# One more batch of a first layer by Strassen's seven products: W1 loaded sooner, two groups of weight sums made later

## The chip, the cores and the metric

The kernel runs on one core of one Trainium2 chip. The metric is the device time of one execution in microseconds (us), as the median of several runs. The engines are named as in the profile: PE is TensorE's matrix multiply and PEld its weight load, DVE is VectorE, ACT is ScalarE, POOL is GpSimd and SP is SyncE, which issues most of the DMAs. A "q" behind a name (SPq, ACTq, POOLq) means the queue from which that engine issues DMAs.

## The reference

Eight batches of 256 tokens with 1024 features pass two layers, each added to its input. All is float32.

```python
# layer 0: mask holds 0 and 1, coeff is one number for each batch
x = x + (x @ W0.T + b0 + (x @ (2 * mask - 1)) * coeff)
# layer 1: a LoRA adapter of rank 16, picked for each batch by itok
x = x + (x @ W1.T + b1 + ((x @ A[itok]) @ B[itok]) * 2.0)
```

The mask differs from batch to batch, so layer 0 has a weight matrix of its own for each batch: W0.T + (2 mask - 1) coeff, with the identity added for the residual. Layer 1 has one weight matrix for all batches, W1.T plus the identity, and a small correction for each batch.

## The kernel before

**Two groups of four batches.** For each group the kernel runs the first layer of its batches one after the other, then the second layer of the whole group (`second_layer`, L613). The results y of a group stay in SBUF, features in rows.

**The first layer, plain.** The effective weights come in pieces of 256 input by 512 output features, eight to a batch. `load` (L171) sends a piece's mask on SP's queue (and W0 in batch 0, and a piece of x with some), four pieces ahead of use. `build` (L209) turns it into weights: one ACT activation computes (2 mask - 1) coeff (L227) and one DVE add puts W0 to it (L230), two pieces ahead of use. Masks have three buffers (pool "mask"), built pieces three as well (pool "weff"). `first_batch` (L271) and `first_layer` (L241) multiply: 64 matmuls of 128 by 128 by 256 for each batch, of which the profile counts two PE records each (L280, L255). Batches 0, 1, 2 and 3 go this way.

**The first layer by seven products.** Batches 4 to 7 (`SEVEN`, L20) use Strassen's method in Winograd's form, class `Seven` (L304): weights are cut in quarters a11, a12, a21, a22, tokens and inputs in halves. Four weight sums s1 to s4 and four token sums t1 to t4 stand in for one of eight quarter products. Each product is made in two halves of eight matmuls with 128 columns (L388), over three PSUM banks X, Y and Z. The order is X: a11; Y: a12; X: s2 t2; Z: s1 t1; X: s3 t3; Z: s4; X: a22 t4, and X and Z are read out between. ACT reads with the bias (L403), DVE adds the others (L408). `operands` (L344) lists the 20 steps that prepare a batch: four blocks a11, a11, a12, a12, then t1 and t2, then twice (a22, a21, s1, s2), then t3, s3 twice, s4 twice and t4. A weight sum is a DVE operation on 128 by 1024 elements (L326), a token sum two of 128 by 256 (L342). `run_one` (L469) keeps the operands ten steps ahead of the halves in the order of the program. The first three blocks of a batch lie in the three weff buffers, the others in pools T and q (L218 to L223).

**The second layer.** It is Strassen twice, one level inside the other: seven outer products A11, A12, S1, S2, S4, S3, A22 (`plan`, L780), each of seven inner products. Its left operands, the leaves, depend on W1 alone. `combine_weights` (L493) makes them in the first layer of group 0: a generator of DVE sums on 128 by 512 elements (L522 to L528, L539), of which `step` (L867) takes three or four after each piece. The leaves are written to HBM on POOL's queue (`keep`, L485) and read back on SP's, seven for each outer product (`load_leaves`, L622). W1's 16 blocks are loaded with the masks of pieces 10 to 21 (L206). The sums S3 are left over and made in the second layer of group 0 (`rest`, L559). `begin_adapters` and `load_adapters` bring the LoRA matrices.

**What sets the order.** The framework orders the instructions of each engine when the kernel is built: by the order of the program among those that it takes to be ready. The engines then keep to that order. `tc.issue_after(ins)` puts instructions behind a given one on its own engine; `behind(what)` does it for the instruction last noted under a name in `anchors`. SBUF pools give a buffer again when its last reader is done. The pools here: mask 3, weff 3, T 6, q 10, l 7 buffers.

```python
if b not in SEVEN or (h == 0 and g < 3):
    pool, tag = wpool, "w"
elif g >= NG // 2:
    pool, tag = tpool, "T"
else:
    pool, tag = qpool, "q"
```

Of the kernel before, what the change touches and what calls it, by code (L numbers as in the profile page):

```python
# [14 lines left out]
P = 128  # L15
# [3 lines left out]
BY_HALF = 3  # L19
SEVEN = (4, 5, 6, 7)  # L20
SCALING = 2.0
# [3 lines left out]
def kernel(  # L25
# [145 lines left out]
    def load(k: int):  # L171


        b, h, g = pieces[k]
        m_sb[k] = mpool.tile([P, 2, OH], I32, tag="m", name=f"m_{k}")
        pairs = [(m_sb[k], mask[b, g if b == 0 else h * NG + g])]
        if b == 0:
            pairs.append((w0_of(k), w0T[g]))
        x_pair = g // CG if b == 0 and g % CG == 0 else g if h == 0 else None
        if x_pair is not None:  # L180
            x = x_sb[b, x_pair] = xpool.tile([P, CG, T], F32, tag=f"x{x_pair}", name=f"x_{b}_{x_pair}")
        if k < BY_HALF:

            for i in range(2):
                for t, a in pairs:
                    nc.sync.dma_start(t[:, i], part(a, i))  # L186
                if k == 0 and i == 0:
                    nc.scalar.dma_start(x[:, 0], part(xT[0, 0], 0))
                elif k == 0:
                    nc.sync.dma_start(x[:, 1], part(xT[0, 0], 1))  # L190
                elif x_pair is not None and i == 0:
                    nc.sync.dma_start(x, xT[b, x_pair])
        else:
            for t, a in pairs:
                nc.sync.dma_start(t, a)
# [12 lines left out]

    def build(k: int):  # L209
# [94 lines left out]
    class Seven:  # L304
# [19 lines left out]
        def weight_sum(self, n, op, x, y, a):  # L324
            s = self.w[n, a] = qpool.tile([P, CG, OH], F32, tag="q", name=f"{n}_{self.b}_{a}")
            anchors["weights"] = op(s, self.w[x, a], self.w[y, a])  # L326
# [50 lines left out]
        def half(self, dest, left, right, a, first=False):  # L377
# [4 lines left out]
            for c in range(CG):  # L382
# [4 lines left out]
                for j in range(TPH):  # L387
                    nc.tensor.matmul(  # L388
                        ps[:, j, :],
# [17 lines left out]
        def add(self, i, v, ps):  # L407
            nc.vector.tensor_add(self.out(i, v), ps, self.out(i, v))  # L408

        def products(self):  # L410
# [38 lines left out]
    class Sevens:  # L449
# [43 lines left out]
    def combine_weights():  # L493
# [17 lines left out]
        def inner(name, blocks, own, place=None):  # L511
            a11, a12, a21, a22 = (blocks[u, v] for u in range(2) for v in range(2))
            s = {}
            for n in ("s1", "s2", "s3", "s4"):
                if place is None:
                    s[n] = lpool.tile([P, CG, OQ], F32, tag="l", name=f"{name}_{n}")
                else:
                    if n in ("s1", "s3"):
                        two = pair(f"{name}_{n}")
                    s[n] = two[:, n in ("s2", "s4")]  # L520
# [13 lines left out]

        def outer(name, op, x, y):
            tiles = [tpool.tile([P, 2, CG, OQ], F32, tag="T", name=f"{name}_{u}") for u in range(2)]
            out = {(u, v): tiles[u][:, v] for u in range(2) for v in range(2)}
            for uv in out:
# [74 lines left out]
    def second_layer(group: int, y, first, first_steps, second):  # L613
# [24 lines left out]
        def product(ps, l, r, first=False, by_tile=False):  # L638
            order = [(c, j) for c in range(CG) for j in range(2)]
            if by_tile:  # L640
                order.sort(key=lambda cj: cj[1])
            for c, j in order:
                nc.tensor.matmul(  # L643
                    ps[:, j, :],
                    lhsT=l[:, c, j * P : (j + 1) * P],
                    rhs=r[:, c, :],
                    start=first and c == 0 and j == 0,
                    stop=False,
                    skip_group_check=True,
                )  # L650

# [40 lines left out]
        def read(out, ps, other=None):  # L692
            if other is None:
                return nc.scalar.copy(out, ps)  # L694
            anchors["reads"] = nc.vector.tensor_add(out, ps, other)  # L695
            return anchors["reads"]
# [170 lines left out]
    def step(k: int):  # L867

        nonlocal sums
        if k == 2 * NG + 3:  # L870
            sums = combine_weights()
        with tc.issue_after(weff_at[min(k + BUILDS_AHEAD, max(weff_at))].ins):
            for _ in range(3 if k < 4 * NG + 2 else 4):
                next(sums, None)

    sevens = {g: Sevens([b for b in SEVEN if b // GB == g]) for g in range(NGROUP)}
    for group in range(NGROUP):
# [19 lines left out]
        for i in range(GB):  # L897
            if GB * group + i in SEVEN:
                continue
            between(GB * group + i)  # L900
            if group == 0 and i == 0:
                first_batch(y[0], step)
                continue
            for h in range(2):
                first_layer(GB * group + i, h, y[i][h], step)
                if group == 0 and i == 2 and h == 0:
                    late = y[i][h][:, 0, :1]
                    begin_adapters(late)
                    load_adapters(group, late)
        for _ in sums:  # L910
            pass
        anchors["layer"] = anchors["weights"]
# [75 lines left out]
```

## Time and profile before

| | |
|---|---|
| median of 3 runs | 410.01 us (409.81 to 411.64) |
| the profiled execution | 410.92 us, its span 409.1 us |
| first layer, group 0 | to 117.8 us in the span |
| second layer, group 0 | 117.8 to 211.4 us |
| first layer, group 1 | 211.4 to 312.0 us |
| second layer, group 1 | from 312.0 us |
| granted TensorE clock | 1.000 |
| DMA, mean | 238 GB/s; 395 GB/s from 60 to 118 us |
| mask, issue to landing, median | 9.2 us from 60 to 118 us, 4.4 us from 211 to 290 us |

The span is the time from the first to the last instruction of one profiled execution. A row of the chain or of the timeline begins with a start and a length in us, both counted from the span's start. "L255 PE MATMUL ps<-x,w ... x384" means 384 PE records of the matmul in line 255, which writes tile ps from x and w. A bracket behind a row gives the idle time of the engine ahead of it and what ended that. Busy time says that an engine had work, not that it set the time; for that the chain of work that ended last is read, which follows each step back to what released it.

### The profile page before, as it was taken

How to read it: one execution, taken by the hardware profiler on the slowest of the kernel's cores; microseconds unless marked ns; L12 is line 12 of the kernel's file. 1: busy time of each engine (PE TensorE's matmuls, PEld its weight loads, DVE VectorE, ACT ScalarE, POOL GpSimd, SP SyncE). 2: the span in 40 equal slices, each digit the busy share in tenths (PEclk: the TensorE clock that was granted, in tenths of full speed). 3: DMA queues.
4: the chain of work that ended last, by engine and by line, in shares of the span. 5: the costliest groups of instructions: out<-in, count | busy, mean ns of one | idle time of the engine just before them, and what ended most of it. 6: DMA issues, size and time to landing. Idle time of an engine off the chain costs nothing.

```text
span 409.1 us, 6555 instructions
## 1 busy us (share of the span) xinstructions
PE 403.8 (99%) x2458; PEld 358.2 (88%) x2458; DVE 300.7 (74%) x427; ACT 136.0 (33%) x213; POOL 38.6 (9%) x77
## 2 busy tenths in 40 slices
PE   8999999999999999999999999999999999999996
PEld 6888888888887888888899999999998788888885
DVE  2438598886647558994999999999936365886493
ACT  4434534543445201133115648174221420102200
POOL 0000042575201001000000000400000000000000
PEclk9999999999999999999999999999999999999999
DMA  8999799999987476767795758662122247554654
GB/s 274 405 402 387 274 371 414 412 393 331 414 331 256 134 234 199 220 218 201 241 367 162 263 184 302 202 215 96 26 74 66 75 145 230 173 154 162 213 154 154
DMA packets 41762, 97.44 MB, mean 238 GB/s; under 512 B 5508, under 2 KB 6276, under 8 KB 41732
## 3 DMA queue, kind: packets, MB, share of 16 engines
q1 hardware_dynamic: 32690, 76.17, 55.2%
q0 software_dynamic: 4288, 12.61, 8.1%
q10 hardware_dynamic: 4754, 8.26, 5.4%
q8 instruction: 19, 0.31, 0.3%
q14 instruction: 11, 0.09, 0.1%
HBM read 77.09 MB, written 19.92 MB: 237 GB/s over the span
## 4 chain that ended last, share of the span: by engine, by line
PE 91%; DMA 5%; ACT 2%; SPq 1%; DVE 0%; issue 0%; DVEq 0%; ACTq 0%
PE X L643 24%; PE ps L255 20%; PE X L388 12%; PE Z L643 12%; PE Z L388 6%; PE Y L643 6%; DMA m<-mask 5%; PE ps L280 4%; PE Y L388 3%; PE G L660 2%; PE psh L675 2%; ACT w L227 1%; ACT y L403 0%; SPq L186 0%; DVE w L230 0%
## 5 line engine op out<-in xcount | busy, mean ns | idle before, releaser
L227 ACT ACTIVATE w<-m,neg_c,two_c 128x1024 f32<-128x1024 int32 (+1 forms) x67 | 80.1, 1203 | 109.9 <-DMA m<-mask 40.7
L230 DVE TENSOR_TENSOR w<-w,w_sb 128x1024 f32<-128x1024 f32 (+1 forms) x67 | 77.4, 1172 | 36.9 <-ACT w L227 32.7
L255 PE MATMUL ps<-x,w 128*128 128x256 f32 x384 | 83.3, 379 | 0.0
L255 PEld LDWEIGHTS ps<-x,w 128*128 128x128 f32 x384 | 72.9, 190 | 10.2 <-DVE w L230 0.4
L778 DVE TENSOR_TENSOR c<-c,e 128x512 f32<-128x512 f32 x48 | 32.0, 683 | 3.9 <-ACT c L669 3.8
L388 PE MATMUL X<-t,s 128*128 128x128 f32 x256 | 30.0, 276 | 0.0
L388 PEld LDWEIGHTS X<-t,s 128*128 128x128 f32 x256 | 29.2, 192 | 0.2 <-ACT y L403 0.2
L280 PE MATMUL ps<-x,w 128*128 128x256 f32 x128 | 28.7, 385 | 0.2 <-DVE w L230 0.2
L669 ACT COPY c<-G 128x512 f32<-128x512 f32 x32 | 16.4, 600 | 36.4 <-PE G L660 33.1
L280 PEld LDWEIGHTS ps<-x,w 128*128 128x128 f32 x128 | 24.8, 194 | 4.2 <-DVE w L230 0.8
L695 DVE TENSOR_TENSOR c<-X,c 128x512 f32<-128x512 f32 (+1 forms) x26 | 16.7, 647 | 15.1 <-PE X L643 15.0
L403 ACT ACTIVATE y<-X,b_sb 128x128 f32<-128x128 f32 x48 | 13.6, 366 | 39.6 <-PE X L388 39.6
L694 ACT COPY e<-X 128x512 f32<-128x512 f32 x16 | 9.4, 588 | 48.0 <-PE X L643 41.7
L643 PE MATMUL X<-T_t,l_S_s 128*128 128x256 f32 x96 | 22.8, 380 | 0.0
L643 PEld LDWEIGHTS X<-T_t,l_S_s 128*128 128x128 f32 x96 | 18.2, 190 | 2.7 <-DVE e L695 0.3
L326 DVE TENSOR_TENSOR s<-w,w 128x1024 f32<-128x1024 f32 x16 | 19.2, 1215 | 0.0
L695 DVE TENSOR_TENSOR e<-X,e 128x512 f32<-128x512 f32 x16 | 10.9, 684 | 6.6 <-PE X L643 6.6
L643 PE MATMUL X<-b_t,l_A_s 128*128 128x256 f32 x64 | 15.5, 386 | 0.0
L388 PE MATMUL Z<-x,s 128*128 128x128 f32 x128 | 15.0, 276 | 0.0
L388 PE MATMUL Y<-x,w 128*128 128x128 f32 x128 | 14.9, 275 | 0.0
L388 PE MATMUL Z<-t,s 128*128 128x128 f32 x128 | 14.9, 275 | 0.0
L388 PE MATMUL X<-t,w 128*128 128x128 f32 x128 | 14.9, 275 | 0.0
(125 smaller groups left out, 622.4 us busy)
## 6 DMA issues: line engine op xcount, KB each, us to landing
m<-mask SPq DMA_DIRECT2D x61, 512.0 KB, 6.1
l_S_s<-leaf_S_s SPq DMA_DIRECT2D x32, 256.0 KB, 2.7
x<-xT SPq DMA_DIRECT2D x31, 256.0 KB, 7.8
outT<-c ACTq DMA_DIRECT2D x30, 256.0 KB, 3.5
l_A_s<-leaf_A_s SPq DMA_DIRECT2D x24, 256.0 KB, 2.7
l_S_a<-leaf_S_a SPq DMA_DIRECT2D x24, 256.0 KB, 2.7
w<-w1T SPq DMA_DIRECT2D x16, 256.0 KB, 6.4
leaf_S_s<-S_s POOLq DMA_DIRECT2D x16, 256.0 KB, 7.0
```

The source lines that it names most:

```text
L227: nc.scalar.activation(w[:, i], m[:, i], AF.Identity, bias=neg_c[:, b : b + 1], scale=two_c[:, b : b + 1])
L230: weff_at[k] = nc.vector.tensor_add(w[:, i], w[:, i], w0_of(k)[:, i])
L255: nc.tensor.matmul(ps[j // 2][:, j % 2, :], lhsT=w[:, c, j * P : (j + 1) * P], rhs=x_sb[b, g][:, c, :],  start=first and j % 2 == 0, stop= ...
L280: nc.tensor.matmul(ps[ot // 2][:, ot % 2, :], lhsT=w[:, h, j * P : (j + 1) * P], rhs=x_sb[0, c // CG][:, c % CG, :], start=c == 0 and ot % ...
L326: anchors["weights"] = op(s, self.w[x, a], self.w[y, a])
L388: nc.tensor.matmul(ps[:, j, :], lhsT=w[:, c, j * P : (j + 1) * P], rhs=r, start=first and a == 0 and c == 0 and j == 0, stop=False, skip_g ...
L403: nc.scalar.activation(self.out(i, v)[:, j, :], ps[:, j, :], AF.Identity, bias=b0_sb[:, ot : ot + 1])
L643: nc.tensor.matmul(ps[:, j, :], lhsT=l[:, c, j * P : (j + 1) * P], rhs=r[:, c, :], start=first and c == 0 and j == 0, stop=False, skip_gro ...
L669: nc.scalar.copy(dest[b // 2][u, b % 2], ps[b])
L694: return nc.scalar.copy(out, ps)
L695: anchors["reads"] = nc.vector.tensor_add(out, ps, other)
L778: nc.vector.tensor_add(o, o, x)
```

## The change

Batch 3 is added to the batches that use seven products. In group 0 the program now runs batches 0, 1 and 2 plain, finishes the weight sums, loads the adapters, and then runs batch 3 by `Sevens.run`. Its first three operand steps are put in behind the last two pieces of batch 2. Its blocks beyond the third all lie in T buffers; s3 and s4 are written over a11 and a12, the first s1 takes a T buffer, the other sums q buffers.

W1's blocks are loaded two to a mask with pieces 8 to 15. `combine_weights` begins two pieces sooner, three sums to a piece, and ends with S4's outer sums, written over A12. S3's outer sums (over A21), S4's inner sums and S3's inner sums come in the second layer of group 0, in T buffers. Several orders are written in: token sums and one add of batch 3 behind the weight sums; the second layer's token sums behind its reads; its first leaf loads behind the last mask; its first products behind those of batch 3.

```diff
-SEVEN = (4, 5, 6, 7)
+SEVEN = (3, 4, 5, 6, 7)
...
-            if k == 2 * NG + 2 + 3 * n // 4:
+            if k == 2 * NG + n // 2:
                 nc.sync.dma_start(raw[q, r], w1T[q, r])
...
-        elif g >= NG // 2:
+        elif g >= NG // 2 or b < GB:
             pool, tag = tpool, "T"
...
         def weight_sum(self, n, op, x, y, a):
-            s = self.w[n, a] = qpool.tile([P, CG, OH], F32, tag="q", name=f"{n}_{self.b}_{a}")
+            if self.b < GB and n in ("s3", "s4"):
+                s = self.w[x, a]
+            elif self.b < GB and n == "s1" and a == 0:
+                s = tpool.tile([P, CG, OH], F32, tag="T", name=f"{n}_{self.b}_{a}")
+            else:
+                s = qpool.tile([P, CG, OH], F32, tag="q", name=f"{n}_{self.b}_{a}")
+            self.w[n, a] = s
             anchors["weights"] = op(s, self.w[x, a], self.w[y, a])
...
-                nc.vector.tensor_sub(o, x, y)
+                with behind("weights") if self.b < GB else nullcontext():
+                    nc.vector.tensor_sub(o, x, y)
...
-            self.add(0, 0, ps["Y"])
+            with behind("weights") if self.b < GB else nullcontext():
+                self.add(0, 0, ps["Y"])
...
             while self.made < early:
-                next(self.operands, None)
+                with behind("layer"):
+                    next(self.operands, None)
...
-        yield from outer("S4", nc.vector.tensor_sub, quads["A12"], quads["S2"])
-        yield from inner("S4", quads["S4"], every)
+        yield from outer("S4", nc.vector.tensor_sub, quads["A12"], quads["S2"], quads["A12"])
         def rest():
-            yield from outer("S3", nc.vector.tensor_sub, quads["A11"], quads["A21"])
-            yield from inner("S3", quads["S3"], every, pair)
+            yield from outer("S3", nc.vector.tensor_sub, quads["A11"], quads["A21"], quads["A21"])
+            yield from inner("S4", quads["S4"], every, two)
+            yield from inner("S3", quads["S3"], every, two)
...
+            with behind("products") if first else nullcontext():
+                for c, j in order:
+                    nc.tensor.matmul(
...
-        rest = chain(*later) if group == 0 else iter(())
-        load_leaves("A11")
+        def ordered(steps):
+            while True:
+                with behind("reads" if "reads" in own else "layer"):
+                    if next(steps, True):
+                        return
+                yield
+        own = {}
+        rest = ordered(chain(*later)) if group == 0 else iter(())
+        with behind("masks"):
+            load_leaves("A11")
         begin(0, "A11", first)
-        for _ in first_steps:
+        for _ in ordered(first_steps):
             pass
...
-            beside=chain(second.sums(), outer_sum(1, b12, b11, "S1")),
+            beside=chain(ordered(second.sums()), outer_sum(1, b12, b11, "S1"), islice(rest, 4)),
...
-        if k == 2 * NG + 3:
+        if k == 2 * NG + 1:
             sums = combine_weights()
-            for _ in range(3 if k < 4 * NG + 2 else 4):
+            for _ in range(3):
                 next(sums, None)
+        if k >= 6 * NG - 2:
+            sevens[0].begin(2 * (k - 6 * NG) + 5)
...
+        if group == 0:
+            first_batch(y[0], step)
+            for b, h in ((1, 0), (1, 1), (2, 0), (2, 1)):
+                first_layer(b, h, y[b][h], step)
+            for _ in sums:
+                pass
+            late = y[2][1][:, 0, :1]
+            begin_adapters(late)
+            load_adapters(group, late)
         sevens[group].run(y, between)
```

More of the change, by code (lines that the diff above doesn't have):

```diff
@@ L175, in load @@
         m_sb[k] = mpool.tile([P, 2, OH], I32, tag="m", name=f"m_{k}")
+        last = (k + 1) % (GB * 2 * NG) == 0
         pairs = [(m_sb[k], mask[b, g if b == 0 else h * NG + g])]
@@ L194, in load @@
             for t, a in pairs:
-                nc.sync.dma_start(t, a)
+                sent = nc.sync.dma_start(t, a)
+            if last:
+                anchors["masks"] = sent
             if x_pair is not None:
@@ L387, in half @@
                 for j in range(TPH):
-                    nc.tensor.matmul(
+                    anchors["products"] = nc.tensor.matmul(
                         ps[:, j, :],
@@ L407, in add @@
         def add(self, i, v, ps):
-            nc.vector.tensor_add(self.out(i, v), ps, self.out(i, v))
+            anchors["weights"] = nc.vector.tensor_add(self.out(i, v), ps, self.out(i, v))
         def products(self):
@@ L518, in inner @@
                     if n in ("s1", "s3"):
-                        two = pair(f"{name}_{n}")
+                        two = place(f"{name}_{n}")
                     s[n] = two[:, n in ("s2", "s4")]
@@ L533, in inner, with two, outer @@
                     keep(name, n, t)
-        def outer(name, op, x, y):
-            tiles = [tpool.tile([P, 2, CG, OQ], F32, tag="T", name=f"{name}_{u}") for u in range(2)]
-            out = {(u, v): tiles[u][:, v] for u in range(2) for v in range(2)}
+        def two(name):
+            return tpool.tile([P, 2, CG, OQ], F32, tag="T", name=name)
+        def outer(name, op, x, y, out=None):
+            if out is None:
+                tiles = [two(f"{name}_{u}") for u in range(2)]
+                out = {(u, v): tiles[u][:, v] for u in range(2) for v in range(2)}
             for uv in out:
@@ L641, in product @@
                 order.sort(key=lambda cj: cj[1])
[L642 to L650, printed above, removed]
+            with behind("products") if first else nullcontext():
+                for c, j in order:
+                    nc.tensor.matmul(
+                        ps[:, j, :],
+                        lhsT=l[:, c, j * P : (j + 1) * P],
+                        rhs=r[:, c, :],
+                        start=first and c == 0 and j == 0,
+                        stop=False,
+                        skip_group_check=True,
+                    )
         def up(i, u, dest):
@@ L694, in read @@
                 return nc.scalar.copy(out, ps)
-            anchors["reads"] = nc.vector.tensor_add(out, ps, other)
+            own["reads"] = anchors["reads"] = nc.vector.tensor_add(out, ps, other)
             return anchors["reads"]
@@ L894, in between @@
                 next(first_steps)
-        sevens[group].run(y, between)
[L897 to L911, printed above, removed]
+        if group == 0:
[7 more added lines that the diff above has]
+            load_adapters(group, late)
+        sevens[group].run(y, between)
         anchors["layer"] = anchors["weights"]
```

## The prediction

> **What bounds the kernel now.** I read the page's engine rows first, then the chain that ended last in order of time, then the busy time by stage, then the timeline around the two places where a first layer begins, and last the DMA landing times.
>
> ```profile
> PE 403.8 (99%) x2458; PEld 358.2 (88%) x2458; DVE 300.7 (74%) x427; ACT 136.0 (33%) x213; POOL 38.6 (9%) x77
> ```
>
> TensorE (PE) is busy 403.8 of 409.1 us, and the other 5.3 us lie in the first 17. From 17.1 us on nothing but PE work sets the time, so work taken from PE there is worth its full length, if PE is fed as well as now. The chain gives the length of a first layer in each form:
>
> ```profile
> 34.66 83.13 PE ps L255 x384
> ...
> 211.41 3.57 PE X L388 x32
> 214.98 3.57 PE Y L388 x32
> 218.56 3.57 PE X L388 x32
> ...
> 312.03 1.73 PE X L643 x8
> ```
>
> Batches 1 to 3 take 83.13 / 3 = 27.71 us each as plain products. Batch 4, by seven products, takes 7 x 3.57 = 25.0 us; all four of group 1 take 312.03 - 211.41 = 100.6, so 25.15 each. So the third batch can give back 27.71 - 25.0 = **2.7 us at most**, 0.66% of the time. (A measurement of this kernel can tell about 0.5%, 2.05 us, from no change.) Next, what the other engines do beside it:
>
> ```profile
> 76.20:90.10 13.90, 13.90 (x65) 11.95 (x64) 12.71 (x21) 5.48 (x6) 9.72 (x19) 1.00 1.03 405
> 90.10:104.00 13.90, 13.90 (x65) 12.25 (x65) 9.54 (x12) 7.36 (x11) 8.14 (x16) 1.00 1.02 343
> 211.40:236.40 25.00, 25.00 (x227) 25.00 (x226) 25.00 (x32) 14.14 (x21) 0.00 (x0) 1.00 0.70 237
> ```
>
> (Columns: stretch, length, PE, PEld, DVE, ACT and POOL busy, clock, DMA share, GB/s.) In a seven-product batch VectorE (DVE) is busy 25.0 of 25.0 us: it is as full as PE. PE waits for nothing there only because batch 4 comes in with a store of operands, as the timeline shows:
>
> ```profile
> 208.60 1.22 DVE L230 TENSOR_TENSOR w<-w,w_sb 128x1024 f32<-128x1024 f32 x1
> ...
> 212.13 1.22 DVE L326 TENSOR_TENSOR s<-s,w 128x1024 f32<-128x1024 f32 x1
> ...
> 217.34 1.22 DVE L326 TENSOR_TENSOR s<-s,w 128x1024 f32<-128x1024 f32 x1
> ...
> 218.39 3.74 PE L388 MATMUL X<-t,s 128*128 128x128 f32 x32
> ```
>
> When PE begins batch 4 at 211.4, DVE has four blocks, t1, t2 and the first a22, a21 and s1 done (the row at 208.60 is a block, the two below it are s2's two sums); five operations of s2 are left, and the last of them (217.34 + 1.22 = 218.56) ends just as PE takes up the s2 product at 218.4. Even with that head start nothing is to spare.
>
> **The change, part by part.** Let t0 = 34.66 + 2 x 27.71 = 90.1 us be the moment when PE ends batch 2.
>
> *Batch 3's products.* 64 plain matmuls go and 112 of half the width come. Here a rule and the row differ. By multiplications alone the batch would shrink to 7/8 of 27.71 = 24.2, a gain of 3.5. [...] The rows show 3.57 / 32 = 112 ns a record, so 25.0. I take the row: 2.7 gained.
>
> *The head start of batch 3.* Here I expect the price. The first three effective blocks (a11 twice, the first a12) use the three weff buffers, which pieces 21, 22 and 23 of batch 2 hold until PE is through them: t0 - 6.9, t0 - 3.5 and t0 (a piece is 27.71 / 8 = 3.46 us). The same was so before:
>
> ```profile
> 90.27 1.55 ACT L267 ACTIVATE y<-ps,b_sb 128x256 f32<-128x256 f32 x4
> ...
> 91.69 1.25 ACT L227 ACTIVATE w<-m,neg_c,two_c 128x1024 f32<-128x1024 int32 x1
> ```
>
> Only this mattered little: a plain layer needs one build per 3.46 us. The seven-product form needs eight builds and four weight sums before its second s2 half, in 8.9 us of PE work (five halves of 1.785). The other blocks lie in T buffers, but each needs one of three mask buffers, which come free as ScalarE (ACT) converts the blocks before them; so the fourth to eighth masks are sent at about t0 - 5.6, t0 - 2.2, t0 + 1.5, t0 + 2.9 and t0 + 4. Masks land in 4.4 us where the DMAs are no fuller than in group 1 (median of 22), 9.2 where they are saturated (median of 16, 60 to 118 us). I take the first, since W1 and seven leaf writes leave this stretch.
>
> DVE's own sum: after t0 it has the third block's add, perhaps the fourth's, four more adds and four sums. With the third block converted by t0 + 1.3 (if ACT takes it before the evacuation) to t0 + 2.9 (91.69 + 1.25 - 90.1, the order of the row above), nine operations of 1.22 = 11.0 and t1 and t2 at 0.75 each = 1.5 follow: the second s2 sum is ready at R between t0 + 13.8 and t0 + 16.6 (with the fourth add after t0). I take R = t0 + 15.2. It is wanted at t0 + 8.9.
>
> What PE makes of the wait depends on its order, which is fixed when the kernel is built. In the order written, nine halves follow R: the batch ends at R + 16.1 = t0 + 31.3, against t0 + 27.7 now: +3.6. If Z's s1 halves are put into the gap, about 14.4 us of PE work and one evacuation are left after R (eight halves less what overlaps): t0 + 29.6, +1.9. Such an interleaving is in the present trace, in a stretch where DVE is full:
>
> ```profile
> 163.83 1.29 PE Y L643 x6
> 165.13 1.87 PE X L643 x8
> 166.99 0.43 PE Y L643 x2
> ```
>
> I take the middle: **+2.7 net** for batch 3, that is 5.4 us of idling less 2.7 saved. Bounds: R = t0 + 13.3 interleaved is 0.0; R = t0 + 17 in written order +5.4. Below zero is reached only if the blocks come well before t0 + 1.
>
> *The clock.* [...] The granted clock is 1.00 in every row here, but from 17.1 us on no row has an idle gap. My gaps are 2 to 4 us, broken by halves of 1.8. By the rows nothing is added[...]. I take nothing[...].
>
> *W1 two blocks a mask, from piece 8.* The same 16 SP issues, earlier, ahead of the masks of batch 1. At most six more blocks stand ahead of a mask than before: 1.6 MB, at 405 GB/s 3.9 us. Masks of 34 to 62 us land in 5.9 us, and a mask can take 5 x 3.46 - 1.24 - 2.5 = 13.6 before PE waits (three buffers, two builds ahead). 5.9 + 3.9 = 9.8: nothing, bound 0 to 2. A gain is excluded, PE waits for no mask there now.
>
> *Weight sums three a step, from piece 9.* 40 sums fit in 14 steps; 3 x 0.69 and a build of 1.22 make 3.3 of 3.46 us. Hidden by builds that run two pieces ahead.
>
> *S4's sums, the rest of first and second sums, S3 in place.* S4's inner four (2.7 us), six T sums (4.1) and part of the two big differences (3.6) go to the second layer: 10.4 us more DVE in its first two products, 117.8 to 151.7, where DVE was busy 13.97 + 6.54 = 20.5 of 33.9. With 31 of 34 it fits; but the c11 and c12 halves that up(0, 1) fills now wait for S3's four sums to free the A11 buffers, behind the last read of the first product. That is 0.7 + 0.7 + 2.4 of DVE and 1.2 of ACT, some 5 us; PE wants the result 8.6 us after. Nothing, bound 0 to 2. S4's leaf writes then have over 20 us until they are read.
>
> *Adapters behind batch 2.* Their three small copies cost DVE 0.5 us after t0 (0.15, 0.14, 0.17 now); 16 DMA issues keep POOL some 11 us, used 20 us later. Nothing, bound 0 to 0.5. *Orders written in.* The first leaf loads go behind group 0's last mask on SP's queue; they wait for the l buffers of t1 to t4, and behind them stand only masks that are used from 211 us on. Y's add goes behind the last s2 sum on DVE: behind it would stand only t3 and the s3 sums, and nobody reads its result before the later add. Both nothing. The second layer's first product goes behind batch 3's products, so that PE can't fill the gap with it; counted above.
>
> Sum: batch 3 +2.7, rest 0. The profiled execution took 410.92 us (span 409.1 and 1.8 around it), 0.9 over the median of the runs; so 413.6 in such an execution and **412.7 us** for the median.
>
> **The rivals.**
> 1. *Late operands, as above*: 412.7, own range 411.5 to 414.5. For it: DVE full in every seven-product batch, weff and mask buffers tied to PE. Chance 46%.
> 2. *The same wait, but better covered*: the fourth block and t1, t2 done before t0, Z's halves in the gap; what is lost equals what is saved: 410.3. Chance 30%.
> 3. *On the other side, not slower*: the T-buffer blocks are built while PE ends batch 2, and the whole 2.7 come: 407.5. It decides at one point: s2's second sum ready by t0 + 8.9 (a quarter of the gain is left at about t0 + 12, interleaved). Against it: at t0 a block is still waiting for its weff buffer, and then 11 us of DVE. Chance 10%.
> 4. *The second layer's start*: DVE, with 10 us more, is late for T1's sums or for c11: 2.5 us on top, 415.2. For it: 31 of 34 us busy. Against: group 1's same stretch runs without a gap. Chance 8%.
> 5. *W1 delays masks in batch 1* by 2 us: 414.7. Chance 6%.
>
> **How the numbers follow.** The likeliest is 412.7. Rival 1 without the tenth of it that lies within 0.5% (42%), 4 and 5 make slower 56%; faster is nine tenths of rival 3, 9%; the rest, 35%, is within 0.5%. The range leaves out rival 3 and the far ends of 1 and 4 (clock, R = t0 + 17): 409.0 to 416.0.
>
> **What would show it.** The new seven-product rows of batch 3 should be 3.57 us where uninterrupted, with PE idle some 5 us between t0 + 7 and t0 + 16, released by DVE's weight sums; DVE full there; batches 1 and 2 unchanged at 27.7; 93.6 us for the second layer as now. I am wrong if at t0 + 7 s1 and s2 are there, if PE's idle time lies elsewhere, or if the clock falls.

## The result, and the profile after

The changed kernel takes **423.0 us** (median of 6 runs, 422.37 to 424.46) against 410.31 us (409.81 to 411.68) for the kernel before in the same comparison: a ratio of 1.0307, 95% interval 1.0281 to 1.0334. It is 12.7 us slower. The prediction was 412.7 us with a range of 409.0 to 416.0: slower, as forecast, but by 12.7 us where 2.7 were expected.

The head of the page, with the engine rows and the row of the granted clock:

```profile
span 422.3 us, 6785 instructions
PE 406.8 (96%) x2554; PEld 362.2 (86%) x2554; DVE 313.1 (74%) x446; ACT 137.4 (33%) x221; POOL 38.5 (9%) x77
PEclk9999999999899998999999999999999999999999
```

PE is idle for 422.3 - 406.8 = 15.5 us, where it was for 5.3. It is also 3.0 us busier, though it has less to do: two slices of the clock row show an 8. The chain of the work that ended last shows where the idle time is:

```profile
78.73 11.62 DMA m<-mask
...
113.37 2.05 PE X L399 x16
...
159.54 3.13 DMA outT<-c
...
196.72 0.61 DVE c L716
197.37 2.00 PE X L664 x8
```

Before, this chain was PE work alone from 17.1 us on. Now it leaves PE four times. Two of these matter: for a mask that was in flight for 11.62 us, and, at 159.54, for a store to HBM. The other two end at 52.26 and at 197.37, on DVE, and PE is idle there for 0.28 and 0.59 us. The stages, by the busy time in each (columns as before: stretch, length, five engines, clock, DMA share, GB/s), first the end of batch 2, then batch 3, then the second layer of group 0:

```profile
76.00:90.80 14.80, 14.51 (x68) 12.46 (x66) 10.44 (x14) 5.50 (x8) 4.67 (x9) 1.00 1.03 415
90.83:126.14 35.31, 28.47 (x225) 27.28 (x226) 24.96 (x32) 16.44 (x26) 9.38 (x18) 0.95 0.74 246
126.14:224.65 98.51, 95.97 (x522) 79.72 (x521) 78.54 (x119) 20.45 (x36) 5.98 (x11) 0.98 0.66 215
```

The last two stages of the kernel before:

```profile
90.10:117.63 27.53, 27.53 (x128) 24.24 (x128) 17.00 (x18) 11.80 (x16) 9.96 (x19) 1.00 1.03 377
117.63:211.25 93.62, 93.62 (x522) 78.69 (x520) 71.22 (x108) 22.97 (x38) 3.78 (x7) 1.00 0.71 226
```

So the 13.2 us between the spans are: batch 3 begins 0.7 later (90.83 for 90.10), takes 7.8 more (35.31 for 27.53), the second layer of group 0 takes 4.9 more (98.51 for 93.62), and the rest, from group 1 on, is 0.2 shorter. Both stages had PE busy from end to end before, and now have idle time and a clock below 1.00. Beyond the 2.7 us that were forecast these are 10.5 us: 5.1 in batch 3, 4.9 in the second layer, 0.7 ahead of them, less the 0.2.

**Batch 3, closer.** Three timelines of the changed kernel. PE:

```profile
90.83 4.22 PE L399 MATMUL X<-x,w 128*128 128x128 f32 x32 [0.32 <-DVE w L233]
96.60 2.05 PE L399 MATMUL Y<-x,w 128*128 128x128 f32 x16 [1.54 <-DVE w L233]
100.43 2.05 PE L399 MATMUL Y<-x,w 128*128 128x128 f32 x16 [1.78 <-DVE w L233]
105.39 2.30 PE L399 MATMUL Z<-t,s 128*128 128x128 f32 x12 [2.91 <-DVE s L336]
107.48 2.90 PE L399 MATMUL X<-t,s 128*128 128x128 f32 x16
...
113.37 2.05 PE L399 MATMUL X<-t,s 128*128 128x128 f32 x16 [0.22 <-DVE s L336]
```

DVE, which makes what PE waits for (L233 adds W0 to a block, L336 are weight sums; those that write w are s3 and s4):

```profile
89.55 1.23 DVE L233 TENSOR_TENSOR w<-w,w_sb 128x1024 f32<-128x1024 f32 x1 [2.31 <-ACT w L230]
...
95.32 1.23 DVE L233 TENSOR_TENSOR w<-w,w_sb 128x1024 f32<-128x1024 f32 x1 [2.17 <-ACT w L230]
99.15 1.23 DVE L233 TENSOR_TENSOR w<-w,w_sb 128x1024 f32<-128x1024 f32 x1 [2.60 <-ACT w L230]
...
101.63 2.35 DVE L233 TENSOR_TENSOR w<-w,w_sb 128x1024 f32<-128x1024 f32 x2
104.02 1.23 DVE L336 TENSOR_TENSOR s<-w,w 128x1024 f32<-128x1024 f32 x1
...
108.69 1.22 DVE L336 TENSOR_TENSOR w<-w,w 128x1024 f32<-128x1024 f32 x1
...
110.96 1.22 DVE L336 TENSOR_TENSOR w<-w,s 128x1024 f32<-128x1024 f32 x1
112.10 1.22 DVE L336 TENSOR_TENSOR s<-s,w 128x1024 f32<-128x1024 f32 x1
```

And ACT, which DVE waits for:

```profile
88.28 1.24 ACT L230 ACTIVATE w<-m,neg_c,two_c 128x1024 f32<-128x1024 int32 x1 [4.71 <-DMA m<-mask]
...
97.88 2.37 ACT L230 ACTIVATE w<-m,neg_c,two_c 128x1024 f32<-128x1024 int32 x2 [1.87 <-DMA m<-mask]
```

The brackets are read backwards: PE waits at 96.60 and 100.43 for blocks from DVE, DVE at 95.32 and 99.15 for ACT, and ACT for masks. The mask of the first block lands at 88.28, so that block is ready at 90.78, the moment when PE wants it, and the third and fourth come at 96.55 and 100.38. Behind the fourth DVE has no idle time any more: t1, t2, two blocks and the first s1 sum take until 105.25, and PE waits 2.91 us for that. At 105.39, 14.6 us into the batch, PE has done four of its fourteen halves, 7.1 us of work.

**The second layer, closer.** ACT's waits of the changed kernel (us in total, times, longest us), and the PE row at that place:

```profile
ACT e L715 <- DMA outT<-c: 18.3, 2, 12.0
```

```profile
163.32 3.08 PE L664 MATMUL X<-T_t,l_S_s 128*128 128x256 f32 x8 [1.96 <-ACT e L715]
```

ACT is to copy a PSUM bank to a tile e, and waits 12.0 us until a store of output c has landed. The chain has the path in full, from PE to PE: PE's product ends at 158.79, DVE finishes c in 0.70 us, the store takes 3.13 (the row at 159.54 above), ACT's copy 0.59. PE waits 1.96 us at the end of it, and 0.75 us later its clock falls to 0.50 (below). The one other gap of this stage is the 0.59 us at 197.37, where PE waits for DVE's c.

### The profile page after: what moved, and what is told of

Its sections match the earlier page's. It is cut to its first block, busy times and chain, and to the rows that moved or that the text cites. A ratio compares the mean times of both kernels' runs of the same rounds, so it can differ in the third digit from the quotient of the medians.

```text
span 422.3 us, 6785 instructions
## 1 busy us (share of the span) xinstructions
PE 406.8 (96%) x2554; PEld 362.2 (86%) x2554; DVE 313.1 (74%) x446; ACT 137.4 (33%) x221; POOL 38.5 (9%) x77
## 4 chain that ended last, share of the span: by engine, by line
PE 79%; DVE 8%; DMA 8%; issue 2%; ACT 1%; SPq 0%; POOL 0%; DVEq 0%; POOLq 0%; ACTq 0%
PE X L664 21%; PE X L399 16%; PE Z L664 10%; PE ps L258 9%; PE Z L399 8%; DMA m<-mask 5%; PE Y L664 5%; PE ps L283 4%; PE Y L399 3%; DVE w L233 2%; PE G L681 2%; PE psh L696 2%; DMA lb_pad<-b 1%; DVE e L716 1%; ACT w L230 1%
## 5 line engine op out<-in xcount | busy, mean ns | idle before, releaser
L233 DVE TENSOR_TENSOR w<-w,w_sb 128x1024 f32<-128x1024 f32 (+1 forms) x67 | 77.2, 1176 | 32.4 <-ACT w L230 31.3
L258 PE MATMUL ps<-x,w 128*128 128x256 f32 x256 | 55.7, 380 | 0.3 <-DVE w L233 0.3
L258 PEld LDWEIGHTS ps<-x,w 128*128 128x128 f32 x256 | 48.7, 190 | 7.1 <-DVE w L233 0.7
L399 PE MATMUL X<-t,s 128*128 128x128 f32 x288 | 34.9, 281 | 0.2 <-DVE s L336 0.2
L399 PEld LDWEIGHTS X<-t,s 128*128 128x128 f32 x288 | 34.0, 197 | 0.4 <-DVE s L336 0.4
L414 ACT ACTIVATE y<-X,b_sb 128x128 f32<-128x128 f32 x60 | 17.1, 364 | 42.5 <-PE X L399 42.5
L283 PE MATMUL ps<-x,w 128*128 128x256 f32 x128 | 28.7, 386 | 0.2 <-DVE w L233 0.2
L283 PEld LDWEIGHTS ps<-x,w 128*128 128x128 f32 x128 | 24.9, 195 | 4.1 <-DVE w L233 0.6
L399 PE MATMUL Z<-t,s 128*128 128x128 f32 x160 | 19.9, 283 | 3.2 <-DVE s L336 3.2
L399 PE MATMUL X<-t,w 128*128 128x128 f32 x192 | 22.5, 276 | 0.0
L399 PE MATMUL Y<-x,w 128*128 128x128 f32 x160 | 19.1, 277 | 3.3 <-DVE w L233 3.3
L399 PEld LDWEIGHTS Z<-t,s 128*128 128x128 f32 x160 | 19.0, 197 | 3.5 <-issue 3.1
L399 PEld LDWEIGHTS X<-t,w 128*128 128x128 f32 x192 | 21.9, 192 | 0.1
L336 DVE TENSOR_TENSOR s<-w,w 128x1024 f32<-128x1024 f32 x18 | 21.7, 1223 | 0.1
L399 PEld LDWEIGHTS Y<-x,w 128*128 128x128 f32 x160 | 18.3, 192 | 3.7 <-DVE w L233 3.7
```

The costliest lines, as they stand in the source:

```text
L233: weff_at[k] = nc.vector.tensor_add(w[:, i], w[:, i], w0_of(k)[:, i])
L258: nc.tensor.matmul(ps[j // 2][:, j % 2, :], lhsT=w[:, c, j * P : (j + 1) * P], rhs=x_sb[b, g][:, c, :],  start=first and j % 2 == 0, stop= ...
L283: nc.tensor.matmul(ps[ot // 2][:, ot % 2, :], lhsT=w[:, h, j * P : (j + 1) * P], rhs=x_sb[0, c // CG][:, c % CG, :], start=c == 0 and ot % ...
L399: anchors["products"] = nc.tensor.matmul(ps[:, j, :], lhsT=w[:, c, j * P : (j + 1) * P], rhs=r, start=first and a == 0 and c == 0 and j == ...
L414: nc.scalar.activation(self.out(i, v)[:, j, :], ps[:, j, :], AF.Identity, bias=b0_sb[:, ot : ot + 1])
```

## The experiments

Four reasons stood against each other. For batch 3: (i) masks land late, because the DMAs are still full; (ii) DVE's chain and the weff buffers, as the prediction had it; (iii) the clock, which fell to 0.50 for 3.4 us after an idle gap of 2.91 us. For the second layer: (iv) DVE has more to do there, against a buffer that comes free late. Each ratio below is to the kernel before, run on the same chip, with its 95% interval; a time like "27.6 us for batch 3" is from the start of its first product to the start of the second layer.

### Batch 3 plain, everything else as changed

```diff
-SEVEN = (3, 4, 5, 6, 7)
+SEVEN = (4, 5, 6, 7)
...
             load_adapters(group, late)
+            between(3)
+            for h in range(2):
+                first_layer(3, h, y[3][h], step)
```

> The changed kernel with batch 3 in the plain form again; W1's early load, the sums left to the second layer and the later adapters stay. Theory A (late operands of batch 3 cost 8.3 us there, and the sums put into the second layer cost 4.9 us there by themselves): 414 to 416 us, the second layer of group 0 still about 98 us long. Theory B (the second layer is long only because batch 3 ends late, with DVE behind): about 410.5 us, second layer 93.6. Theory C (W1's early load delays plain batches too): above 417.

Measured: 413.95 us, 1.0076 (1.0057 to 1.0095). The second layer begins at 118.69 and takes 96.1 us, 2.5 more than before: between the two theories. So the other edits cost about 3 us by themselves, and the seven products of batch 3 about 9.

### No masks for batch 3

The first try built batch 3's blocks from the last mask of batch 2, which was kept:

```diff
-        m_sb[k] = mpool.tile([P, 2, OH], I32, tag="m", name=f"m_{k}")
+        if b == 3:
+            m_sb[k] = kept[0]
+        else:
+            m_sb[k] = mpool.tile([P, 2, OH], I32, tag="m", name=f"m_{k}")
+        if k == 6 * NG - 1:
+            kept.append(m_sb[k])
...
-        pairs = [(m_sb[k], mask[b, g if b == 0 else h * NG + g])]
+        pairs = [] if b == 3 else [(m_sb[k], mask[b, g if b == 0 else h * NG + g])]
```

> The changed kernel without the eight mask loads of batch 3: its blocks are built from the last mask of batch 2, so batch 3's result is another one; all other work stays. Theory A (the masks of batch 3 land late, because the DMAs are full): batch 3 shrinks from 36 to 28 to 30 us, time 415 to 417. Theory B (the weff buffers and DVE's own chain of blocks and sums make it late): batch 3 stays at 33 us or more, time 420 or more.

Measured: 421.27 us, 1.0234 (1.0205 to 1.0262). (The test's masks are all ones, so the result was the same after all.) Batch 3 took 26.3 us, but batch 2 ended 6 us late, after an idle gap of 3.79 us on PE, behind which 32 PE records took 9.76 us (36 ahead of it took 7.93): one of three mask buffers was held, and ACT's order was another. That delay was the experiment's own doing, and gave batch 3 a head start, so it decides nothing. The second try builds the blocks from W0, which lies in SBUF, and holds no mask buffer:

```diff
-        m_sb[k] = mpool.tile([P, 2, OH], I32, tag="m", name=f"m_{k}")
+        m_sb[k] = w0_of(k) if b == 3 else mpool.tile([P, 2, OH], I32, tag="m", name=f"m_{k}")
...
-        pairs = [(m_sb[k], mask[b, g if b == 0 else h * NG + g])]
+        pairs = [] if b == 3 else [(m_sb[k], mask[b, g if b == 0 else h * NG + g])]
```

> The changed kernel without batch 3's mask loads, this time with nothing held back: its blocks are built from W0 in the mask's place, so batch 3's result is another one, and no mask buffer is used by it. ACT and DVE do the same operations. Theory A (masks late in full DMAs): batch 2 ends at 90.5 as before, batch 3 takes 27 to 30 us in place of 36, time 414 to 417. Theory B (weff buffers and DVE's chain): batch 3 33 us or more, time 419 or more.

Measured: 415.52 us, 1.0110 (1.0076 to 1.0145), as theory A had it. Batch 3, then the second layer, by stage:

```profile
90.41:117.99 27.58, 25.79 (x225) 25.30 (x224) 21.66 (x27) 11.42 (x21) 9.42 (x18) 1.00 0.54 178
117.99:215.81 97.82, 94.37 (x523) 78.26 (x521) 78.48 (x119) 20.68 (x37) 6.02 (x11) 1.00 0.66 214
```

Batch 3 is 7.7 us shorter and as long as the plain one was, at full clock. One wait for a block is left in it:

```profile
95.94 3.84 PE L399 MATMUL Y<-x,w 128*128 128x128 f32 x32 [1.67 <-DVE w L233]
```

It is the third block, the one in the last weff buffer. The masks are the 7.7 us; the weff buffer is 1.7. The second layer has hardly changed (97.82), so its loss is another matter. Since it ran at full clock and still took 97.82, half the clock is not what it lost first: PE waits 2.86 us for ACT's e there.

### Nine leaf writes fewer

Nine of the leaves of S1, S2 and S4 are plain copies; here they are not written, and W1 is read in their place. The DVE sums are all made.

```diff
-                if n in own:
+                if n in own and name in ("S1", "S2", "S4"):
+                    leaf_at[name, n] = w1T[0, 0]
+                elif n in own:
                     keep(name, n, t)
```

> The changed kernel without the nine leaf writes that only copy a quarter of S1, S2 and S4 (2.4 MB, 5.8 us of full DMAs, most of them between 62 and 90 us); the second layer reads a W1 block in their place, so its result is another one. Masks, buffers and DVE work stay. Theory A (the leaf writes that share the DMAs make the masks late): masks land up to 5 us sooner, batch 3 takes 30 to 33 us, time 417.5 to 420.5. Theory B (mask buffers that come free late, not the DMAs): 422 to 424.

Measured: 419.53 us, 1.0206 (1.0155 to 1.0257); batch 3 takes 30.45 us, 4.9 less, as theory A had it. The DMA queues from 62 to 97 us (packets, MB, share of 16 engines; then the mask loads: count, KB, median us from issue to landing) of the kernel before, the changed one, and this experiment:

```profile
q1 hardware_dynamic: 3257, 8.46, 64.8%
q0 software_dynamic: 1902, 5.11, 38.1%
...
m<-mask SPq DMA_DIRECT2D x10, 512.0 KB, 9.6
```

```profile
q1 hardware_dynamic: 2843, 7.85, 56.1%
q0 software_dynamic: 2088, 6.64, 46.9%
...
m<-mask SPq DMA_DIRECT2D x9, 512.0 KB, 8.5
```

```profile
q1 hardware_dynamic: 3114, 8.79, 66.4%
q0 software_dynamic: 1490, 4.32, 30.7%
...
m<-mask SPq DMA_DIRECT2D x11, 512.0 KB, 5.9
```

q1 is SP's loads, q0 POOL's writes. The change did take loads out of this stretch (8.46 to 7.85 MB), but POOL wrote 1.5 MB more in it. The shares add up to 103% before and after, so a mask took nearly as long as ever. With nine writes fewer the shares add up to 97% and a mask lands in 5.9 us.

Where the added writes come from is seen in the kernel before, beside its batch 3 (90.1 to 117.6 us):

```profile
leaf_S_s<-S_s POOLq DMA_DIRECT2D x8, 256.0 KB, 8.7
leaf_S_a<-S POOLq DMA_DIRECT2D x6, 256.0 KB, 9.4
```

These fourteen leaves were written while batch 3 ran. The changed kernel finishes the sums of the first layer ahead of batch 3, and writes no leaf from 90.8 to 126.1 us: four of the fourteen (S4's inner sums) have gone to the second layer, and ten have come forward, so that 33 leaves are written before batch 3 instead of 23.

### W1 as before; then only the sums as before

```diff
-            if k == 2 * NG + n // 2:
+            if k == 2 * NG + 2 + 3 * n // 4:
...
-        if k == 2 * NG + 1:
+        if k == 2 * NG + 3:
...
-            for _ in range(3):
+            for _ in range(3 if k < 4 * NG + 2 else 4):
```

> The changed kernel with W1 loaded and the sums begun as before (pieces 10 to 21, sums from piece 11, three and then four a step). Theory A (the DMAs are full up to batch 3 whatever the order, since all the bytes have to pass before it): batch 3's masks land as late, 421 to 425 us. Theory B (the early W1 pushes leaf writes into the masks' way): masks land sooner, below 420 us.

Measured: 430.13 us, 1.0472 (1.0439 to 1.0505); a mask lands in 10.7 us, batch 3 takes 38.8. That is above what either theory allowed. The other experiment has only the last two of these three edits:

> The changed kernel with W1 loaded early, but the sums begun as before (from piece 11, three and then four a step). It parts e3_w1late's 7 us. Theory A (leaf writes nearer to batch 3 push its masks back): 426 to 430. Theory B (the W1 blocks among batch 2's masks did it): 422 to 424.5.

Measured: 424.74 us, 1.0335 (1.0290 to 1.0380), batch 3 38.2 us. This lies between the two theories. Loading W1 sooner is good for about 5.4 us of the 7.1; the 1.7 that are left for the early sums are not clear of the noise, since this interval overlaps that of the changed kernel. So it is not the early start of the sums that fills the DMAs: begun as before, the sums still have all 33 leaves written before batch 3, only closer to it.

### S4's inner sums in the first layer, as before

```diff
         yield from outer("S4", nc.vector.tensor_sub, quads["A12"], quads["S2"], quads["A12"])
+        yield from inner("S4", quads["S4"], every)
...
-            yield from inner("S4", quads["S4"], every, two)
```

> The changed kernel with S4's four inner sums back in the first layer of group 0 (its outer sums stay in A12's place), so that only S3 is left to the second layer. Theory A (S4's sums and the q buffers that A12 holds for them make the second layer long): its stretch falls from 98.5 to about 95, and the time to 418.5 to 421. Theory B (S3's sums and the late T sums do it): second layer 98, time 423 or, with four more leaf writes among the masks, more.

Measured: 422.31 us, 1.0283 (1.0252 to 1.0314). ACT waits 6.3 us for a store, as in the kernel before, PE waits for nothing there, and the second layer takes 93.94 us, within 0.3 of what it took before. But batch 3 takes 37.1 us, 1.8 more. Four more leaf writes lie ahead of it, and the four sums stand ahead of the second block's add on DVE, where PE waits 1.62 us; how the 1.8 divide between these two was not tested. The stage did as theory A said; the time did not, and is not clear of that of the changed kernel.

### The store taken off the buffer

The tile e that ACT waits for takes a buffer of pool q from c11, which must first be stored. Here e1, which is not in the way, is stored in c11's place (that part of the output is then not the layer's result), so c11's buffer comes free when DVE has read it. Nothing else moves: DVE has the same work.

```diff
-                    store(out[uv], *dest, *uv)
+                    store((e1 if n == 1 and group == 0 else out)[uv], *dest, *uv)
```

> The changed kernel in which the second outer product of group 0 stores e1's quarters in place of c11's (as many bytes, but a wrong quarter of the output), so that c11's q buffers come free without waiting for a store. Theory A (e5 waits for a q buffer until c11's store has landed, because A12 and A21 hold four of them for S4 and S3): the wait of ACT at 160 us goes, with the half clock after it; second layer 95 to 96.5 us, time 419.5 to 421.5. Theory B (DVE's added sums are the reason): second layer 98, time 423.

Measured: 420.59 us, 1.0234 (1.0217 to 1.0252), batch 3 in 35.66 us, and the second layer:

```profile
126.82:221.43 94.61, 94.02 (x523) 78.42 (x522) 78.45 (x119) 20.78 (x37) 5.99 (x11) 1.00 0.71 224
```

3.9 of the 4.9 us are gone with DVE as busy as before (78.45), so it was the buffer and not DVE. (The 3.9 hold the half clock that followed the gap, too.) Why the buffer is short: S4 and S3 now lie over A12 and A21, so these keep four q buffers into the second layer.

### S4's inner sums ahead of S3's outer ones

```diff
         def rest():
-            yield from outer("S3", nc.vector.tensor_sub, quads["A11"], quads["A21"], quads["A21"])
             yield from inner("S4", quads["S4"], every, two)
+            yield from outer("S3", nc.vector.tensor_sub, quads["A11"], quads["A21"], quads["A21"])
```

> The changed kernel with the order of the left-over sums in the second layer turned round: S4's inner sums in the first outer product, S3's outer sums in the second, so that the buffers of A12 come free first and those of A11 in time for e5. Nothing is left out. Theory A (e5's buffers): the wait of ACT at 160 us goes, second layer 95 to 97, time 420 to 422. Theory B (DVE's added sums): second layer 98 and more.

Measured: 422.34 us, 1.0259 (1.0223 to 1.0294); the second layer takes 97.3 us, 1.2 less. The wait of ACT did not go, as theory A had it: ACT still waits 12.54 us for the store, until 164.02. The trace no longer puts a wait of PE to it, but PE waits 1.05 us for a leaf of S to be read back, and 0.74 and 0.95 for DVE's c. This order, which leaves all of the work in place, gives back a quarter of the loss at most, since the stage also ran at full clock this time (eight records in 1.89 to 1.97 us behind that place, where the changed kernel took 3.08).

### The gap filled

Six matmuls whose result nobody reads go behind the Y halves, and the later halves of batch 3 behind them, to keep PE busy while it waits for the first s1 sum.

```diff
+                    with behind("fill") if self.b < GB else nullcontext():
+                        anchors["products"] = nc.tensor.matmul(
...
+            if self.b < GB:
+                fill = psum.tile([P, T], F32, tag="ps", name="fill_ps")
+                with behind("products"):
+                    for _ in range(FILL):
+                        anchors["fill"] = nc.tensor.matmul(
+                            fill, lhsT=ident, rhs=w0_sb[:, 0, :T], start=True, stop=True
+                        )
```

> The changed kernel with six idle matmuls (2.6 us, result unused) between the Y halves and the s1 and s2 halves of batch 3, so that PE is not idle in the longest gap and its clock should stay at 1.00 from 105 to 110 us. Theory A (DVE's chain sets the pace there, the lost clock is covered by it): 422.5 to 424. Theory C (the half clock after the gap costs its full 1.7 us): 421 to 422.

Measured: 426.02 us, 1.0353 (1.0320 to 1.0387), batch 3 38.0 us. The fillers closed the gap they were put in, but PE took the later halves in another order and a gap of 2.13 us came later; the clock fell there (0.50 from 113 to 115 us):

```profile
105.85 0.91 PE L401 MATMUL Z<-t,s 128*128 128x128 f32 x6 [0.32 <-DVE s L337]
...
112.38 3.48 PE L401 MATMUL Z<-t,s 128*128 128x128 f32 x16 [2.13 <-DVE s L337]
```

This settles nothing about the price of the clock, since the drop was moved and not removed.

### The third block, and all hindrances together

The third block of batch 3 takes a mask buffer, which lies free once batch 3 needs no masks (blocks from W0 again, as above):

```diff
-        if b not in SEVEN or (h == 0 and g < 3):
+        if b == 3 and h == 0 and g == 2:
+            pool, tag = mpool, "m"
+        elif b not in SEVEN or (h == 0 and g < 3):
             pool, tag = wpool, "w"
```

> As e5_nomask (blocks of batch 3 built from W0, no mask loads), and the third block, the first a12, is built into a free mask buffer instead of the weff buffer that PE holds to the end of batch 2. Batch 3's result is another one. Theory B (the third weff buffer is what is left of the wait): the 1.7 us wait before the Y product goes, batch 3 takes 25 to 26 us, 2 us less than e5_nomask: about 413.5. Theory D (DVE's chain would be late next): batch 3 stays at 27 us or more and the wait moves to s1 or s2.

Measured: 414.81 us, 1.0087 (1.0046 to 1.0128), batch 3 26.66 us, 0.9 less than with masks alone taken out: less than theory B hoped for. The wait for the third block is gone, and one for DVE's second s2 sum has come:

```profile
103.74 2.05 PE L401 MATMUL X<-t,s 128*128 128x128 f32 x16 [1.38 <-DVE s L338]
```

This is the wait that the prediction had in mind; it is the last in the row, not the first. With S4's inner sums in the first layer besides:

> As e9_third_block, with S4's inner sums in the first layer too (as in e4_s4early). If masks, third block and q buffers are all that the change pays with, batch 3 takes 25 to 26 and the second layer 94 us: 1.5 us below the kernel before, about 409.5. If the early W1 or the DVE work costs something besides, it is above it.

Measured: 411.75 us, 1.0011 (0.9999 to 1.0023), by stage from the start of batch 3:

```profile
90.17:117.52 27.35, 26.14 (x226) 25.38 (x224) 22.67 (x32) 10.30 (x20) 11.02 (x21) 1.00 0.63 215
117.52:211.45 93.93, 93.93 (x523) 78.59 (x522) 75.85 (x115) 20.45 (x37) 3.83 (x7) 1.00 0.68 214
```

Masks, third block and second layer are all out of the way, and the kernel is as fast as before, no faster, where 409.5 was expected: of the 2.7 us that seven products save, 1.2 go in idle gaps (0.64 of them for the second block's add, which stands behind S4's sums on DVE) and 1.1 in rows that are longer than 3.57. In the first part of batch 3 DVE is the limit:

```profile
86.80:109.00 22.20, 20.99 (x165) 19.82 (x164) 22.04 (x31) 9.72 (x20) 12.10 (x23) 1.00 0.71 255
```

It is busy 22.04 of 22.20 us. No version beat the kernel before, even with the masks left out.

## Why the prediction was right on the sign and wrong on the size

*What bounds the kernel.* Right: PE alone set the time before, and every us in which it idles or is slowed now shows in the time: 13.2 in the span, 12.7 in the median.

*Batch 3's products, 2.7 gained.* Right as a size where nothing interrupts them: group 1's rows are still 3.57 us, 112 ns a record. In batch 3 they were not uninterrupted. Of the 35.31 us 28.47 are busy, and of these 25.0 are products, 1.7 the clock, and the other 1.8 rows that are longer after a gap or where halves alternate between banks (a half of 2.05 where 3.57 / 2 = 1.79). What part is which was not separated.

*The head start of batch 3, +2.7 net.* **This is the first step that failed**, in one term: "I take the first, since W1 and seven leaf writes leave this stretch", a landing time of 4.4 us for the masks that was measured in group 1, in place of the 9.2 of the stretch itself. The stretch did not empty: of the writes beside the old batch 3 four left, not seven, and ten came forward, because the change has all the leaf sums of the first layer done before batch 3. They filled with 1.5 MB of writes what the loads had left, and the masks took 8.5 us, up to 13.3. So PE's first operand came at t0 and not before, the third block was converted at t0 + 4.5 (95.3) where t0 + 1.3 to t0 + 2.9 had been allowed, the fourth at t0 + 8.3, and the second s2 sum was ready at R = t0 + 22.5 (113.32 on a t0 of 90.83), not at t0 + 15.2. Of these 7.3 us some five may be put to the masks, by a sum and not by a run: the difference of the two landing times, 9.2 - 4.4 = 4.8, would have given R = t0 + 20. The other 2.3 are s3's and s4's first sums, which stand ahead of the second s2 sum on DVE (108.69 and 110.96, 1.14 us each from start to start) and which the working left out; PE waited 0.27 us for the second s1 sum and 0.22 for the second s2 sum behind them, so they cost little. Without masks batch 3 takes 27.58 us, as much as the plain one. The experiments with nine writes fewer (-4.9 us at a landing of 5.9) and with W1 late (+3.5 at 10.7) bear on the same term from both sides; with the nine writes out, batch 3 takes 30.45 us, the 30.4 of the prediction.

The interleaving was better than the middle that was taken: Z's two s1 halves and X's first s2 half ran before R, and only 12.8 us of the batch came after it, where 15.2 were counted. That gave 2.4 back; 7.3 - 2.4 = 4.9 us is what batch 3 took beyond the 30.4 that the prediction's steps make.

*DVE full, weff buffers tied to PE.* Both true, and both were second. As waits of their own they appear only once the masks are gone: 1.67 us for the third block, then 1.38 for the second s2 sum. In the experiment that frees everything they eat the 2.7 us, which is the prediction's second rival (410.3, cover equal to loss), with the masks taken away.

*The clock, nothing taken.* Wrong: it fell twice. Two stretches of the changed kernel ran at half the rate. They begin 0.66 us after PE came back from the gap of 2.91 us and 0.75 us after it came back from that of 1.96:

```profile
106.05:109.46 3.41, 3.41 (x19) 3.41 (x18) 3.41 (x4) 1.24 (x1) 0.00 (x0) 0.50 1.06 254
164.07:167.49 3.42, 3.42 (x10) 2.71 (x9) 0.69 (x1) 0.58 (x1) 0.00 (x0) 0.50 0.58 216
```

Each is 3.4 us at 0.50, so 1.7 us of PE work. The kernel before has no idle gap on PE from 17.1 us on, so its trace could not show what a gap does; to take nothing was the author's estimate. What the half clock alone costs stays open, since PE waited for operands around it in any case: the second layer took 97.82 us at full clock without masks, and 98.51 with the drop. Nor do the six runs of the changed kernel follow their mean clock: the one at 1.000 took 423.31 us, the one at 0.986 took 422.37.

*W1 two blocks a mask, nothing.* Right that nothing is seen of a cost; its being early is worth some 5.4 us against W1 late with the same batch 3.

*Weight sums three a step, nothing.* Right for DVE and PE: batches 1 and 2 took their time to within 0.7 us. Their writes, though, are the ones that kept the DMAs full; the step counted their DVE time and not their DMAs.

*The second layer, "nothing, bound 0 to 2".* Wrong, +4.9; **this is the second step that failed**. DVE's added work (10.4 us as counted, 78.54 - 71.22 = 7.3 in the stage) did fit: with the one buffer freed, the same DVE work lies in a stage of 94.61. The step looked at the tile that S3's sums delay, and not at the next tile to take a buffer from the same pool: e, on ACT, behind the store of c11. The fourth rival (the second layer's start, 2.5 us) had the place, not the cause; the run that frees that one buffer gives back 3.9 of the 4.9, and the one that has S4 done in the first layer, so that A12's buffers come free sooner, 4.6.

*Adapters, orders written in.* Right within 0.7: batch 3 began at 90.83, and no PE row waits for an adapter.

## What to carry to other kernels

A form that needs its operands sooner needs its transfers sooner: price each by the landing time of the stretch in which it runs, and take a better one only after the bytes of that stretch have been added up, with all that the edit moves into it; work that must now be done before a stage brings its transfers with it. Where a buffer is held longer, name every later tile that takes one from that pool and what sets the one before free, an output's store included. A saving of 2.7 us that needs a second engine full from its first moment has no reserve; the same form gained in batches 4 to 7 because these came with their operands made.

## What the runs showed of the hardware

PE's clock fell to half after some idle gaps and not after others. The idle gap on PE, and the clock 1 us after its end:

| kernel, start of the gap | gap, us | clock 1 us after it |
|---|---|---|
| changed, 102.5 | 2.91 | half |
| changed, 161.4 | 1.96 | half |
| gap filled, 110.2 | 2.13 | half |
| W1 as before, 100.7 | 4.45 | half |
| W1 as before, 113.9 | 2.73 | full |
| changed, 98.7 | 1.78 | full |

The clock fell behind gaps of 1.96, 2.13, 2.91 and 4.45 us and not behind those of 1.78 and 2.73, so among these six length alone does not decide. Both drops of the changed kernel lasted 3.4 us. In the 3.41 us right ahead of the first (102.64 to 106.05) PE was busy for 0.66 us, in those ahead of the second for 1.45:

```profile
160.66:164.07 3.41, 1.45 (x7) 0.95 (x6) 1.85 (x4) 0.58 (x1) 1.89 (x4) 1.00 0.94 329
```

What decides between such gaps was not shown.

The 16 DMA engines were full at 415 GB/s, and loads and writes shared that, 56% to 47% of their time; under it a load of 512 KB took 8.5 us in the median and up to 13.3 to land (62 to 97 us), and 5.9 in the median where the shares added up to 97% (nine leaf writes fewer). Larger pools of masks or weff buffers, which might have started the masks sooner, were not tried.
